# A window-attention and Fourier kernel: score buffers, first loads and score banks rearranged

## The chip, the cores and the metric

The kernel runs on one core of a Trainium2 chip. Everything is float32. The metric is the device time of one execution in microseconds (us), lower is better; before the change the runs shown have a median of 3386.23 us (3383.5 to 3388.03, three runs). The engines go by short names: PE is the matmul engine, DVE the vector engine, ACT the scalar engine, POOL is GpSimd, and SP issues DMAs. ACT and POOL can issue DMAs too. Matmul results land in PSUM, eight banks of 128 partitions by 512 floats, from where DVE and ACT evict them; POOL works on the main on-chip memory alone.

## What is computed

32 images of 56 x 56 tokens with 128 channels go through two residual layers, each behind a group normalization (32 groups of 4 channels).

```python
# layer 0: shifted-window attention, windows of 7 x 7, shift 3, 4 heads of 32 channels
x = x + L0(gn(x))
    xs   = roll(x, (-3, -3));  win = windows of 49 tokens, 8 x 8 of them an image
    q, k, v = win @ w_qkv.T                      # per head, q scaled by 32 ** -0.5
    attn = softmax(q @ k.T + bias[head] + mask[window])
    out  = roll((attn @ v) @ w_proj.T + b_proj, (3, 3))
# layer 1: Fourier mixing along both axes, then a feed-forward of 512
x = x + L1(gn(x))
    xy = idct(dct(x, W)[:32] mixed by w0);  xx = idct(dct(x, H)[:32] mixed by w1)
    out = relu((xx + xy) @ W1 + b1) @ W2 + b2
```

## The kernel before, in words

The program is one long loop over cycles. A cycle starts one row of eight windows, 392 tokens; eight rows make an image, so 256 rows in all. The order of the instructions on PE, ACT, DVE and POOL is written out by hand: what the loop calls first stands first on its engine, and each engine works strictly in that order. DMAs stand in their issuer's order.

**The attention of a row** is spread over several cycles. `attn_qk` (L393) makes the q and k products of row r in one PSUM bank each, and ACT evicts them, q once (L406) and k twice (L416, for even and odd heads). `attn_scores` (L438) makes 16 matmuls into two banks; DVE adds the bias and the mask while it evicts them into a score buffer `a` (L459). `attn_max` (L466) takes the row maximum on DVE (L469) and subtracts it on POOL (L470); `attn_exp` (L474) is one ACT instruction. `attn_recip` and `attn_divide` (L478, L486) sum and invert on DVE and divide on POOL, in six pieces (L495), into `blocks`; `attn_transpose` (L502) turns these on DVE into `eT` (L505). `attn_v` (L424) makes v of the row, evicted by ACT (L436). `attn_values` (L508) multiplies by v into two banks, evicted by ACT (L552) and DVE (L550). `attn_project` (L554) projects into one bank, and DVE adds the input rows while it evicts (L569) and SP stores the result to a scratch in memory. `attn_sums` (L579) forms group sums on DVE and squares on ACT (L593).

**PSUM.** There are two rings of banks, each handed out in turn: `pa` with four banks for the attention (L81) and `pc` with four for the Fourier layer and the feed-forward (L84). A tile from a ring may be written only when what was read from the same bank last has been read. In the steady part a cycle takes eight banks from `pa`, in this order: q, k, two for the values, two for the scores, v, projection.

**The opening.** Image 0 is loaded in eight DMAs, half by SP and half by ACT, each of 32 rows by 56 tokens by 32 channels (`load_columns_of`, L130); `turn_quarter` (L296) transposes it on DVE, a quarter at a time. Then come constants, the bias table (seven small DMAs into `rpb_cols`, seven more into `rpb`, one copy of it to the upper half of the partitions, L180 to L187), four mask DMAs (L195), and on DVE the sum of both, `bm` (`bias_and_mask`, L201, L205). `image_norm` (L336) is a chain of small DVE instructions with one POOL instruction, the inverse deviation (L377), from which ACT scales the weights (L385); every q product waits for that.

**The first rows.** For cycles 0 to 10 (`CONV_BEGIN` is 11) `first_rows` (L1031) sets the order. In cycle c it calls: q and k of row c, exponential of row c-1, values of row c-3, bias of the input rows, division of row c-1, transposition of row c-2, scores and maximum of row c, projection of row c-3, steps of the next image's normalization, sums of row c-4, loads, v of row c, the mask additions on POOL (cycles 4 and 5), and the next image's quarter.

**The steady part.** From cycle 11 on, `halves_first` (L894), `half_columns`, `eighths`, `quarters`, `behind_max` and `halves_last` (L1003) interleave the Fourier layer and the feed-forward of earlier images with the attention of row c. On PE a cycle runs q and k (in `halves_first`), the first feed-forward product, values, scores, pieces of the Fourier layer, v, more of these, the second feed-forward product, and last the projection (in `halves_last`); right behind it stand q and k of the next row. On DVE the eviction of the second feed-forward product (L811, whose input needs an addition by POOL, L783) stands ahead of the eviction of the projection (L569).

Of the kernel before, what the change touches and what calls it, by code (L numbers as in the profile page):

```python
# [14 lines left out]
P = 128  # L15
# [31 lines left out]
def swin_fourier_kernel(  # L47
# [30 lines left out]
    def bank(tag, bufs):  # L78
        return psum.tile([P, HB], F32, tag=tag, name=tag, bufs=bufs)

    def attn_bank():  # L81
        return bank("pa", 4)

    def conv_bank():  # L84
        return bank("pc", 4)
# [41 lines left out]

    HW = S // 2

    def load_columns_of(dst, b, k, w0, w1, both=False):  # L130
        rows = slice(k * (S - KB), k * (S - KB) + KB)
        for cb in range(C // KB):
            cs = slice(cb * KB, (cb + 1) * KB)
            (nc.scalar if both and cb % 2 else nc.sync).dma_start(dst[cs], x[b, rows, w0:w1, cs])

    def load_quarter(b, k, u):

        t = work.tile([P, HW, KB], F32, tag="xin", name="xin", bufs=1)
        load_columns_of(t, b, k, u * HW, (u + 1) * HW)
        return t  # L140

    xins = {}
    for k in range(2):
        first = big.tile([P, NM * S + JP - S], F32, tag="y", name="xin_first", bufs=2)
        first = first[:, : S * KB].rearrange("p (w c) -> p w c", w=S)
        load_columns_of(first, 0, k, 0, S, True)
        for u in range(2):
            xins[0, k, u] = first[:, u * HW : (u + 1) * HW]
    x1 = big.tile([TC, NCH, C], F32, tag="x1", name="x1")


# [19 lines left out]
    with nc.allow_non_contiguous_dma(reason="relative position bias, once"):  # L171


        cols = work.tile([P, 4, C], F32, tag="zT", name="rpb_cols").rearrange("p n c -> p (n c)")
        cols = cols[:WS, : NH * span * WS].rearrange("p (h y x) -> p h y x", h=NH, y=span)
        for ix in range(WS):
            src = bass.AP(
                rpb_rev.tensor, rpb_rev.offset + WS - 1 - ix, [[span, NH * span], [1, WS]]
            )
            (nc.scalar if ix % 2 else nc.sync).dma_start(  # L180
                cols[ix : ix + 1].rearrange("p h y x -> p (h y) x"), src.unsqueeze(0)
            )
        for iy in range(WS):
            nc.sync.dma_start(
                rpb[iy * WS : (iy + 1) * WS], cols[:, :, WS - 1 - iy : span - iy]
            )
    nc.sync.dma_start(rpb[JP : JP + WT], rpb[0:WT])  # L187
# [4 lines left out]
    for hh in range(2):  # L192
        rows = slice(hh * JP, hh * JP + WT)
        for k, src in enumerate((shift_mask[:, 0, 0:WT], shift_mask[:, 2, JP : JP + WT])):
            nc.sync.dma_start(mask_sb[rows, :, k], src.rearrange("r p j -> p r j"))  # L195
    NP = NWR // 2
    bm = const.tile([P, 2, 2, NP, 2, WT], F32, tag="bm", name="bm")
    nc.gpsimd.memset(bm, 0.0)
# [70 lines left out]
    nc.vector.memset(heads, 0.0)  # L269
    for h in range(NH):  # L270
        nc.vector.memset(heads[h * HD : (h + 1) * HD, h % 2 : h % 2 + 1], 1.0)
    q_sb = big.tile([P, RT + JP - WT], F32, tag="q", name="q")
    nc.gpsimd.memset(q_sb, 0.0)
    v_sb = [big.tile([P, NP, C], F32, tag=f"v{i}", name=f"v{i}") for i in range(3)]
    a_sb = [big.tile([P, NH, NP, WT], F32, tag=f"a{i}", name=f"a{i}") for i in range(2)]
    blocks = [
        big.tile([P, 2, NH * NP, KB], F32, tag=f"blocks{i}", name=f"blocks{i}") for i in range(2)
    ]
# [2 lines left out]

    class Image:
        pass
# [49 lines left out]
    def image_norm(im):  # L336
# [47 lines left out]
        )  # L384
        nc.scalar.mul(im.w, wqkv, rstd)  # L385
        yield
        pb = attn_bank()
        halved(pb[:, 0:1], wqkv[:, 2 * C :], nb)
        nc.vector.tensor_copy(im.bias[:, 2:3], pb[:, 0:1])
        yield  # L390
# [46 lines left out]

    def attn_scores(im, i, r):  # L438

        q, a = q_sb, a_sb[r % 2]  # L440

        ps = [attn_bank(), attn_bank()]
        for pr in range(NP):
            for hp in range(2):
                cs = HALVES[hp]
                for e in range(2):
                    w = 2 * pr + e  # L450
                    nc.tensor.matmul(  # L451
                        ps[hp][HALVES[e], pr * 2 * WT : (pr + 1) * 2 * WT],
                        lhsT=q[cs, w * WT : w * WT + JP],
                        rhs=k_sb[cs, :, w],
                        start=True,
                        stop=True,
                    )
        for hp in range(2):
            nc.vector.tensor_tensor(  # L459
                a[:, 2 * hp : 2 * hp + 2, :, 0:WT].rearrange("p u w j -> p w u j"),  # L460
                ps[hp][:, :RT].rearrange("p (w u j) -> p w u j", u=2, j=WT),
                bm[:, i // (NWR - 1), hp],
                ALU.add,
            )

    def attn_max(r):  # L466
        a3 = a_sb[r % 2].rearrange("p t w j -> p (t w) j")
        mx = small.tile([P, 2 * NWR], F32, tag="mx", name="mx")
        nc.vector.tensor_reduce(mx, a3, axis=AX.X, op=ALU.max)  # L469
        nc.gpsimd.tensor_tensor(  # L470
            a3, a3, mx.unsqueeze(2).to_broadcast([P, 2 * NWR, WT]), ALU.subtract
        )

    def attn_exp(r):  # L474
        a2 = a_sb[r % 2].rearrange("p t w j -> p (t w j)")
        nc.scalar.activation(a2, a2, AF.Exp)  # L476

    def attn_recip(r):  # L478
        a3 = a_sb[r % 2].rearrange("p t w j -> p (t w) j")
        sm = small.tile([P, 2 * NWR], F32, tag="sm", name="sm")  # L480
        nc.vector.tensor_reduce(sm, a3, axis=AX.X, op=ALU.add)  # L481
        rs = small.tile([P, 2 * NWR], F32, tag="rs", name="rs")
        nc.vector.reciprocal(rs, sm)  # L483
        return rs

    def attn_divide(r, rs):  # L486
        a3 = a_sb[r % 2].rearrange("p t w j -> p (t w) j")
        dst = blocks[r % 2]
        lo, hi = (slice(0, KB), slice(KB, JP)), (slice(JP, JP + KB), slice(JP + KB, P))
        halves = [(slice(0, P), slice(0, P), k, k) for k in range(2)]  # L490
# [115 lines left out]
            )  # L606

    def fourier_stats(im):
        pg = attn_bank()

        for k, t in enumerate((im.tot, im.part[:, NWR - 1])):
            t = t.rearrange("p k g -> p (k g)")
# [417 lines left out]

    def first_rows(cycle):  # L1031
        im, i = row(cycle)
        if im:
            attn_qk(im, i)
        if cycle:
            attn_exp(cycle - 1)
        im3, i3 = row(cycle - 3)
        if im3:
            attn_values(im3, i3, cycle - 3)
        tokens_bias(cycle)  # L1040
        divide(cycle)
        turn(cycle)
        if im:
            attn_scores(im, i, cycle)
            attn_max(cycle)
        if im3:
            attn_project(im3, i3)
        for _ in range(3 if cycle == NWR - 1 else cycle in (0, NWR)):
            norm_step(cycle)
        last, j = row(cycle - 4)  # L1050
        if last:
# [114 lines left out]
```

## Time and profile before

| what | value |
|---|---|
| median of the runs shown | 3386.23 us (3383.5 to 3388.03) |
| the profiled execution | 3378.94 us, of which the span 3377.1 us |
| granted PE clock, mean | 0.99 |
| chain that ended last | PE 78%, DVE 8%, POOL 5%, ACT 5%, issue 3%, DMA 1% |
| scores: L451, 32 matmul records a row | 8192, 251 ns each |
| eviction of scores: L459 | 512, 560 ns each |
| row maximum: L469 | 256, 967 ns each |
| subtraction on POOL: L470 | 256, 1508 ns each |
| exponential: L476 | 256, 855 ns each |
| division on POOL: L495 | 1536, 856 ns each |

The slices of the page show the opening as the only stretch in which PE isn't full:

```profile
PE   4689999999999999999999999999999999999999
PEld 2467777777878777777777777777777777777776
DVE  6778777777777777777778777777777778777641
ACT  2456665566655666666666665566665666665553
POOL 5777777677676777777777676677776777777641
PEclk8889999999999999999999999999999999999999
```

Each digit is a fortieth of the span (84 us) and gives the busy share in tenths; the last line is the clock that PE was granted. Matmuls are pipelined and their ends are modelled, so a busy PE says that there was always a matmul under way, not that each ran at its best.

### The profile page before, as it was taken

To read this page: it belongs to the slowest core of one execution; us is meant where nothing else is said; L and a number is where in the kernel's file an instruction comes from. 1 tells how busy PE (TensorE), PEld (TensorE's weight loads), DVE (VectorE), ACT (ScalarE), POOL (GpSimd) and SP (SyncE) were. 2 spreads that over 40 slices of the span, in tenths; PEclk is the share of its full clock that TensorE was granted. 3 is DMA by queue.
4 is the path that set the end of the run, shared out by engine and by line. 5 is a ranking of instruction groups with operands and counts; after the bars stand their busy time and mean duration, and the time that the engine had idled before them with its cause. 6 is when DMAs were issued, how large, how long until landed. Compare 5 with 4: busy or idle time off the path is not lost.

```text
span 3377.1 us, 158257 instructions
## 1 busy us (share of the span) xinstructions
PE 3252.4 (96%) x69504; PEld 2561.5 (76%) x69504; DVE 2468.8 (73%) x4793; ACT 1979.1 (59%) x3649; POOL 2334.6 (69%) x2724
## 2 busy tenths in 40 slices
PE   4689999999999999999999999999999999999999
PEld 2467777777878777777777777777777777777776
DVE  6778777777777777777778777777777778777641
ACT  2456665566655666666666665566665666665553
POOL 5777777677676777777777676677776777777641
PEclk8889999999999999999999999999999999999999
DMA  5546555556555555555556555555555655555443
GB/s 94 111 117 149 134 132 139 130 136 147 131 132 132 141 133 142 140 133 137 137 137 147 134 133 131 135 135 141 135 139 134 140 137 140 138 135 132 117 129 101
DMA packets 1158097, 448.85 MB, mean 133 GB/s; under 512 B 509951, under 2 KB 1127584, under 8 KB 1157408
## 3 DMA queue, kind: packets, MB, share of 16 engines
q1 hardware_dynamic: 1149565, 437.50, 54.2%
q8 instruction: 546, 8.95, 1.2%
q10 hardware_dynamic: 7843, 1.24, 0.3%
q14 instruction: 143, 1.17, 0.1%
HBM read 277.01 MB, written 161.48 MB: 130 GB/s over the span
## 4 chain that ended last, share of the span: by engine, by line
PE 78%; DVE 8%; POOL 5%; ACT 5%; issue 3%; DMA 1%; SPq 0%; DVEq 0%; POOLq 0%; ACTq 0%
PE pc L110 36%; PE pa L110 13%; PE pa L429 6%; PE pc L666 5%; PE pc L739 5%; PE pa L451 5%; PE pa L520 4%; PE pc L700 4%; POOL blocks L495 4%; ACT hid L776 2%; POOL a L470 1%; DVE eT L505 1%; DVE a L459 1%; DVE xw L308 1%; DVE st L329 1%
## 5 line engine op out<-in xcount | busy, mean ns | idle before, releaser
L495 POOL TENSOR_TENSOR blocks<-a,rs 32x512 f32<-32x512 f32 (+3 forms) x1536 | 1304.3, 856 | 646.9 <-DVE rs L483 542.4
L110 PE MATMUL pc<-wff,hid 128*64 128x128 f32 x12544 | 744.2, 273 | 2.5 <-issue 1.0
L110 PE MATMUL pc<-xf,wff 128*64 128x512 f32 (+2 forms) x3584 | 720.1, 539 | 1.1 <-DVE xf L750 0.9
L110 PEld LDWEIGHTS pc<-wff,hid 128*64 128x64 f32 x12544 | 705.0, 137 | 10.5 <-ACT hid L776 4.6
L110 PEld LDWEIGHTS pc<-xf,wff 128*64 128x64 f32 x3584 | 291.4, 136 | 344.1 <-issue 229.7
L470 POOL TENSOR_TENSOR a<-a,mx 128x784 f32<-128x784 f32 x256 | 386.0, 1508 | 235.4 <-DVE mx L469 202.5
L776 ACT ACTIVATE hid<-pc,b1sb 128x512 f32<-128x512 f32 (+2 forms) x896 | 512.9, 646 | 60.7 <-PE pc L110 52.6
L550 DVE TENSOR_SCALAR oT<-pa,bqkv 128x147 f32<-128x147 f32 (+2 forms) x768 | 171.1, 279 | 376.1 <-PE pa L520 376.1
L593 ACT ACTIVATE xr<-x 112x384 f32<-112x384 f32 (+1 forms) x256 | 147.1, 574 | 509.5 <-DVE x L569 509.5
L110 PE MATMUL pa<-xw,wn 128*64 128x392 f32 x2048 | 400.8, 500 | 41.3 <-ACT wn L385 36.2
L811 DVE TENSOR_TENSOR res<-pc,res 128x512 f32<-128x512 f32 (+3 forms) x257 | 143.0, 566 | 373.6 <-issue 168.3
L436 ACT COPY v<-pa 128x512 f32<-128x512 f32 x256 | 152.1, 594 | 356.4 <-PE pa L429 356.1
L783 POOL TENSOR_TENSOR res<-res,b2sb 128x512 f32<-128x512 f32 (+2 forms) x256 | 266.8, 1048 | 88.2 <-DMA res<-scr 88.2
L416 ACT ACTIVATE k<-pa,bqkv,heads 128x392 f32<-128x392 f32 x512 | 317.5, 673 | 2.3 <-PE pa L110 1.9
L476 ACT ACTIVATE a<-a 128x784 f32<-128x784 f32 x256 | 218.8, 855 | 170.4 <-POOL a L470 160.4
L505 DVE STREAM_TRANSPOSE eT<-blocks 128x1024 f32<-128x1024 f32 x256 | 315.7, 1233 | 0.0
L429 PE MATMUL pa<-wn,xw 128*64 128x128 f32 x4096 | 290.1, 283 | 15.9 <-issue 7.8
L124 POOL TENSOR_TENSOR xr<-xr,bproj 112x384 f32<-112x384 f32 (+1 forms) x256 | 292.5, 1142 | 7.4 <-DMA xr<-in_x_dram 7.3
L459 DVE TENSOR_TENSOR a<-pa,bm 128x392 f32<-128x392 f32 x512 | 265.2, 560 | 30.1 <-PE pa L451 6.5
L520 PEld LDWEIGHTS pa<-eT,v 49*32 49x32 f32 x16384 | 173.7, 106 | 146.5 <-issue 94.7
L110 PE MATMUL pa<-wproj,oT 128*48 128x128 f32 (+1 forms) x3584 | 253.3, 276 | 21.7 <-ACT oT L552 15.4
L481 DVE TENSOR_REDUCE sm<-a 128x16 f32<-128x784 f32 x256 | 245.2, 958 | 35.6 <-ACT a L476 35.5
(94 smaller groups left out, 5023.0 us busy)
## 6 DMA issues: line engine op xcount, KB each, us to landing
zscr<-z SPq DMA_DIRECT2D x512, 112.0 KB
xin<-in_x_dram SPq DMA_DIRECT2D x496, 112.0 KB
htok<-scr SPq DMA_DIRECT2D x256, 196.0 KB
zT<-zscr SPq DMA_DIRECT2D x192, 256.0 KB
res<-scr SPq DMA_DIRECT2D x160, 256.0 KB
out_dram<-res SPq DMA_DIRECT2D x160, 256.0 KB
scr<-x SPq DMA_DIRECT2D x128, 224.0 KB
xr<-in_x_dram SPq DMA_DIRECT2D x128, 168.0 KB
```

Source lines behind the costliest of these rows:

```text
L110: nc.tensor.matmul(dst[ps], lhsT=lhsT[:, ps], rhs=rhs, start=start, stop=stop)
L124: nc.gpsimd.tensor_tensor(piece, piece, bproj.unsqueeze(1).to_broadcast([TC, n, C]), ALU.add)
L416: nc.scalar.activation(k_sb[:, u], pk[:, :RT].rearrange("p (w j) -> p w j", j=WT), AF.Identity, bias=im.bias[:, 3 + u : 4 + u], scale=head ...
L429: nc.tensor.matmul(pv[HALVES[w % 2], w // 2 * C : (w // 2 + 1) * C], lhsT=im.half[i // NP][:, t0 : t0 + JP], rhs=im.w[:, 2 * C : 3 * C], s ...
L459: nc.vector.tensor_tensor(a[:, 2 * hp : 2 * hp + 2, :, 0:WT].rearrange("p u w j -> p w u j"), ps[hp][:, :RT].rearrange("p (w u j) -> p w u ...
L470: nc.gpsimd.tensor_tensor(a3, a3, mx.unsqueeze(2).to_broadcast([P, 2 * NWR, WT]), ALU.subtract)
L481: nc.vector.tensor_reduce(sm, a3, axis=AX.X, op=ALU.add)
L495: nc.gpsimd.tensor_tensor(dst[to, k, :, :n], a3[src, :, kb * KB : kb * KB + n], rs[src].unsqueeze(2).to_broadcast([src.stop - src.start, 2 ...
L505: nc.vector.transpose(eT.rearrange("p t (k j) -> p k t j", k=2), blocks[r % 2])
L520: nc.tensor.matmul(po4[u][h * HD : (h + 1) * HD, pr], lhsT=v[ks, pr, h * HD : (h + 1) * HD], rhs=eT[ks, h * NP + pr, :WT], start=True, sto ...
L776: nc.scalar.activation(hf[:, :n], ph[:, :n], AF.Relu, bias=b1sb[:, f : f + 1])
L783: nc.gpsimd.tensor_tensor(im.res[:m, c0:c1], im.res[:m, c0:c1], b2sb[:m].unsqueeze(1).to_broadcast([m, c1 - c0, C]), ALU.add,)
```

## The change

Five things are changed at once.

1. *Three score buffers in the first rows, and another order there.* A third buffer, `a_extra`, is laid into space that the loads of image 0 leave. Rows 0 to 8 go round three buffers, later ones round two. In `first_rows` the scores, the maximum with its subtraction, and now also the exponential of row c stand ahead of the division of row c-1. The mask additions move from POOL in cycles 4 and 5 to DVE in cycles 1 and 2, and two of image 1's normalization steps move from cycle 7 to the end of cycle 6.
2. *Image 0 in quarters.* Sixteen DMAs of half the size in place of eight.
3. *Small loads by GpSimd.* The bias table's and the mask's DMAs are issued by POOL in place of SP and ACT.
4. *Banks.* The scores get two banks of their own, `ps0` and `ps1`, cleared once; the ring `pa` goes from four banks to two. The two small products of the normalizations are taken from `pc`.
5. *49 weight columns.* The score matmuls load 49 columns of q in place of 64; the partitions between the windows stay zero from the one clearing, and q's tile loses its padding.

In the steady part the order of the calls is untouched. The built program places the first group of `bm` additions on DVE between the second and the third quarter of image 0, the second group between the third and the fourth, and POOL's DMAs between its clear of `bm` and its other clears.

```diff
     def attn_bank():
-        return bank("pa", 4)
+        return bank("pa", 2)
...
-    def load_columns_of(dst, b, k, w0, w1, both=False):
+    def load_quarter(b, k, u):
+        if b:
+            t = work.tile([P, HW, KB], F32, tag="xin", name="xin", bufs=1)
+        elif u:
+            t = others[k]
+        else:
+            t = big.tile([P, NM * S + JP - S], F32, tag="y", name="xin_first", bufs=2)
+            t = t[:, : S * KB].rearrange("p (w c) -> p w c", w=S)
+            others.append(t[:, HW:])
+            t = t[:, :HW]
         rows = slice(k * (S - KB), k * (S - KB) + KB)
         for cb in range(C // KB):
             cs = slice(cb * KB, (cb + 1) * KB)
-            (nc.scalar if both and cb % 2 else nc.sync).dma_start(dst[cs], x[b, rows, w0:w1, cs])
+            queue = nc.scalar if b == 0 and cb % 2 else nc.sync
+            queue.dma_start(t[cs], x[b, rows, u * HW : (u + 1) * HW, cs])
...
-            (nc.scalar if ix % 2 else nc.sync).dma_start(
+            nc.gpsimd.dma_start(
                 cols[ix : ix + 1].rearrange("p h y x -> p (h y) x"), src.unsqueeze(0)
...
-            nc.sync.dma_start(
+            nc.gpsimd.dma_start(
                 rpb[iy * WS : (iy + 1) * WS], cols[:, :, WS - 1 - iy : span - iy]
...
-    nc.sync.dma_start(rpb[JP : JP + WT], rpb[0:WT])
+    nc.gpsimd.dma_start(rpb[JP : JP + WT], rpb[0:WT])
...
-            nc.sync.dma_start(mask_sb[rows, :, k], src.rearrange("r p j -> p r j"))
+            nc.gpsimd.dma_start(mask_sb[rows, :, k], src.rearrange("r p j -> p r j"))
...
-    q_sb = big.tile([P, RT + JP - WT], F32, tag="q", name="q")
-    nc.gpsimd.memset(q_sb, 0.0)
+    q_sb = big.tile([P, RT], F32, tag="q", name="q")
...
+    def attn_buffer(r):
+        return a_sb[r % 3 if r < CONV_BEGIN - 2 else r % 2]
...
+    ps = [bank(f"ps{hp}", 1) for hp in range(2)]
+    for t in ps:
+        nc.vector.memset(t, 0.0)
...
-        pb = attn_bank()
+        pb = conv_bank()
...
-        ps = [attn_bank(), attn_bank()]
...
-                        ps[hp][HALVES[e], pr * 2 * WT : (pr + 1) * 2 * WT],
-                        lhsT=q[cs, w * WT : w * WT + JP],
+                        ps[hp][e * JP : e * JP + WT, pr * 2 * WT : (pr + 1) * 2 * WT],
+                        lhsT=q[cs, w * WT : (w + 1) * WT],
...
-        pg = attn_bank()
+        pg = conv_bank()
...
     def first_rows(cycle):
         im, i = row(cycle)
+        im3, i3 = row(cycle - 3)
         if im:
             attn_qk(im, i)
-        if cycle:
-            attn_exp(cycle - 1)
-        im3, i3 = row(cycle - 3)
         if im3:
             attn_values(im3, i3, cycle - 3)
         tokens_bias(cycle)
-        divide(cycle)
-        turn(cycle)
         if im:
             attn_scores(im, i, cycle)
             attn_max(cycle)
+            attn_exp(cycle)
+        divide(cycle)
+        turn(cycle)
...
-        for _ in range(3 if cycle == NWR - 1 else cycle in (0, NWR)):
+        for _ in range(cycle in (0, NWR - 1, NWR)):
             norm_step(cycle)
...
-        if cycle in (4, 5):
+        if cycle in (1, 2):
             for half in range(2):
-                bias_and_mask(nc.gpsimd, 1, cycle - 4, half)
+                bias_and_mask(nc.vector, 1, cycle - 1, half)
...
+        if cycle == NWR - 2:
+            for _ in range(2):
+                norm_step(NWR - 1)
...
         if cycle == CONV_BEGIN - 1:
             attn_sums(im3, i3)
-            attn_exp(cycle)
...
+        extra = big.tile([P, NM * S + JP - S], F32, tag="y", name="a_extra", bufs=2)
+        extra = extra[:, : NH * NP * WT].rearrange("p (t w j) -> p t w j", t=NH, w=NP)
+        a_sb.append(extra)
```

More of the change, by code (lines that the diff above doesn't have):

```diff
@@ L133, in load_columns_of @@
             cs = slice(cb * KB, (cb + 1) * KB)
-            (nc.scalar if both and cb % 2 else nc.sync).dma_start(dst[cs], x[b, rows, w0:w1, cs])
-    def load_quarter(b, k, u):
-        t = work.tile([P, HW, KB], F32, tag="xin", name="xin", bufs=1)
-        load_columns_of(t, b, k, u * HW, (u + 1) * HW)
+            queue = nc.scalar if b == 0 and cb % 2 else nc.sync
+            queue.dma_start(t[cs], x[b, rows, u * HW : (u + 1) * HW, cs])
         return t
-    xins = {}
+    xins, others = {}, []
     for k in range(2):
-        first = big.tile([P, NM * S + JP - S], F32, tag="y", name="xin_first", bufs=2)
-        first = first[:, : S * KB].rearrange("p (w c) -> p w c", w=S)
-        load_columns_of(first, 0, k, 0, S, True)
         for u in range(2):
-            xins[0, k, u] = first[:, u * HW : (u + 1) * HW]
+            xins[0, k, u] = load_quarter(0, k, u)
     x1 = big.tile([TC, NCH, C], F32, tag="x1", name="x1")
@@ L438, in attn_scores @@
     def attn_scores(im, i, r):
-        q, a = q_sb, a_sb[r % 2]
-        ps = [attn_bank(), attn_bank()]
+        q, a = q_sb, attn_buffer(r)
         for pr in range(NP):
@@ L466, in attn_max @@
     def attn_max(r):
-        a3 = a_sb[r % 2].rearrange("p t w j -> p (t w) j")
+        a3 = attn_buffer(r).rearrange("p t w j -> p (t w) j")
         mx = small.tile([P, 2 * NWR], F32, tag="mx", name="mx")
@@ L474, in attn_exp @@
     def attn_exp(r):
-        a2 = a_sb[r % 2].rearrange("p t w j -> p (t w j)")
+        a2 = attn_buffer(r).rearrange("p t w j -> p (t w j)")
         nc.scalar.activation(a2, a2, AF.Exp)
     def attn_recip(r):
-        a3 = a_sb[r % 2].rearrange("p t w j -> p (t w) j")
+        a3 = attn_buffer(r).rearrange("p t w j -> p (t w) j")
         sm = small.tile([P, 2 * NWR], F32, tag="sm", name="sm")
@@ L486, in attn_divide @@
     def attn_divide(r, rs):
-        a3 = a_sb[r % 2].rearrange("p t w j -> p (t w) j")
+        a3 = attn_buffer(r).rearrange("p t w j -> p (t w) j")
         dst = blocks[r % 2]
```

## The prediction

> **What bounds the kernel now.** I read the page's busy shares first, then the stretches, then the timeline of one image, then the opening 60 us.
>
> ```profile
> PE 3252.4 (96%) x69504; PEld 2561.5 (76%) x69504; DVE 2468.8 (73%) x4793; ACT 1979.1 (59%) x3649; POOL 2334.6 (69%) x2724
> ```
>
> ```profile
> 142.00:200.00 58.00, 44.11 (x966) 36.18 (x963) 46.42 (x93) 28.69 (x56) 41.80 (x50) 0.83 0.52 119
> 200.00:260.00 60.00, 54.98 (x1268) 42.93 (x1266) 45.64 (x86) 34.08 (x62) 41.99 (x51) 0.94 0.55 118
> 1600.00:1705.00 105.00, 104.74 (x2286) 80.99 (x2282) 81.42 (x161) 65.86 (x122) 76.00 (x88) 1.00 0.57 137
> ```
>
> The columns are stretch, length, then busy time of PE, weight loads, DVE, ACT and POOL, granted clock, DMA share, GB/s. In the middle of the run PE is busy 104.74 of 105 us at clock 1.00; only ahead of about 260 us does it idle. Two consequences. A wait put in front of PE in the steady part is paid in full; and work saved in the opening is worth its own length once.
>
> Now the seam between two window rows in the steady part: the projection of one row (PE, `pa<-wproj,oT`), its eviction (DVE L569), and the q and k products of the next row (PE, `pa<-xw,wn`, q first).
>
> ```profile
> 1625.55 1.04 PE L110 MATMUL pa<-wproj,oT 128*64 128x128 f32 x16
> 1626.42 1.49 PE L110 MATMUL pa<-xw,wn 128*64 128x392 f32 x8
> 1626.64 0.69 DVE L569 TENSOR_TENSOR x<-pa,xr 112x512 f32<-112x512 f32 x1
> ...
> 1645.83 1.04 PE L110 MATMUL pa<-wproj,oT 128*64 128x128 f32 x16
> 1646.70 1.49 PE L110 MATMUL pa<-xw,wn 128*64 128x392 f32 x8
> 1648.03 3.60 PE L110 MATMUL pc<-xf,wff 128*64 128x512 f32 x16
> ...
> 1648.14 0.42 DVE L811 TENSOR_TENSOR res<-pc,res 128x256 f32<-128x256 f32 x1 [1.22 <-POOL res L783]
> 1648.48 0.68 DVE L569 TENSOR_TENSOR x<-pa,xr 112x512 f32<-112x512 f32 x1
> ```
>
> Columns: start, duration, engine, line, operation. PE goes from one to the next without a gap, and the eviction runs beside the q and k products: it ends at 1627.33 and at 1649.16, while the k product starts 0.66 after the q product (an image's first row, where another matmul lies between the two, shows q at 1611.08 and that matmul at 1611.74), so at 1627.08 and 1647.36.
>
> **The change, part by part.**
>
> *Two shared banks in place of four.* A window row takes, in the steady order, banks for q, k, two value products, v and the projection: after the change six from a ring of two, as the score products have banks of their own. So q takes the bank that v left, k the one that the projection left. The k product must then wait for L569. Before, k took the bank of a score product, emptied long ago. The eight rows of the image above give, as end of L569 less start of k: 0.03, 0.25, 0.31, 1.80, 0.15, 0.25, 0.25, 0.60 us, 3.64 together. The 1.80 is DVE held for 1.22 by POOL's L783, ahead of L569. Over rows 24 to 255 (images 3 to 31), by the same subtraction, the mean is 3.36 per image. A release from DVE to PE adds its hop: a transpose that ends at 48.36 (47.17 + 1.19) lets PE start at 48.50, so 0.15 each, 1.2 per image. Behind k on PE stand the feed-forward, value and score products, and all wait too. What comes back: PE waits for ACT between scores and v in four of the eight rows, 0.11, 0.11, 0.11 and 0.23 us over the usual 0.73; ACT's backlog there shrinks when PE comes later, so I return 0.45 of these 0.56. Net 3.36 + 1.2 - 0.45 = 4.1 us per image, x 29 = **119 us**. Bounds: no hop and twice the return, 2.4 x 29 = 70; all of 3.64 + 1.2 and no return, 4.84 x 29 = 140. The other new waits are covered: q waits for v's copy on ACT, which ended 1.68 us or more ahead of q in every row from 24 on; the value products now wait for k's eviction, 0.1 to 1.9 us ahead of them, and k is late by no more than PE is. If that cover were gone, the tightest row would pay 0.1 us, 3 us in all.
>
> In rows 11 to 23 the subtraction gives 19.6 us, but PE was busy only 76% and 92% of the two stretches above. I count **6**; bounds 0 and 22 (with hops).
>
> The clock: the stretches grant 0.79 on average from 40 to 120 us, where PE idles for several us at a time, and 1.00 where it is dense; new waits of 0.2 to 1.9 us lie between, and I count no loss of clock. [...]
>
> *49 weight columns for the scores.* Per row 32 weight loads and 32 matmul records.
>
> ```profile
> L110 PE MATMUL pa<-wproj,oT 128*48 128x128 f32 x1792 | 243.1, 277 | 0.0
> L110 PE MATMUL pa<-wproj,oT 128*64 128x128 f32 x1792 | 242.1, 276 | 21.7 <-ACT oT L552 15.4 <-DVE oT L550 6.3
> ```
>
> The groups by shape show that 48 and 64 weight columns cost a matmul the same (277 and 276 ns, the number behind the busy time); only the load shortens, 124 against 139 ns, and PE hides loads. I take 0. If the score block of 0.73 us shrank by 15/64, it would give back 0.17 x 232 rows = 40 us; that is the other end.
>
> *Small loads by GpSimd.* Nineteen DMAs (7 bias columns, 4 masks, 7 rearrangements, 1 copy) go from SP and ACT to POOL, in its order behind `bm`'s clear (ends at 2.1) and ahead of its other clears and of L377, the inverse deviation that opens the matmuls. SP and ACT lose them, which nothing waits for. The two clears of the score banks on DVE fall before 9.97 us, where it waits for image 0 anyway (0.84 to 1.7 us is all it does there); without that cover they would cost about 1 us, by `blocks`' clears of 0.95 on POOL.
>
> ```profile
> 11.66 4.70 SPq L180 DMA_DIRECT2D rpb_cols<-in_rpb_rev_dram  x4
> 18.47 5.82 SPq L184 DMA_DIRECT2D rpb<-rpb_cols  x7
> ...
> 23.58 0.56 POOL L377 TENSOR_TENSOR rstd<-ve,mhalf 128x1 f32<-128x1 f32 x1 [19.01 <-DVE ve L373]
> ...
> 25.95 0.80 SPq L187 DMA_DIRECT2D rpb<-rpb  x1
> ```
>
> The additions into `bm` (L205, two groups of 1.45 us) now stand between image 0's quarters on DVE, so the transposes queue behind them and they behind POOL's DMAs. No row shows a DMA issued by POOL. With p for an issue: 18 issues end at 2.1 + 18p; 2.2 us of clears and landing, the copy p, its landing 2.6 (from 26.75 to the additions at 29.33); then 1.45 of additions, 1.8 and 2.0 of last quarter and statistics, 2.6 of normalization: L377 at 14.8 + 19p. Nearest row: SP issues the same transfers at 0.83 (5.82/7): 0.8 gives 30.0 against 23.58, a **loss of 6.4**. Bounds: at 0.25 (the shortest small load on SP) DVE's own work is the limit, near 25, a loss of 1.5; at 2.07 (the longest, image 0's loads, 8.27/4) it is 54, a loss of 30. Image 0 in quarters is inside this: transposes may begin up to 4 us ahead of 9.97, but they stand behind the additions.
>
> *First rows.* Before, score evictions follow each other at 9.24 and 9.31 us (57.51, 66.75, 76.06), with two long beats, 14.3 (76.06 to 90.33; a quarter's DMA awaited until 84.09, POOL adding masks for 2.9) and 15.9 (99.57 to 115.43; image 1's normalization). Afterwards POOL needs 8.4 per row (division 5.34, subtraction 1.50, 1.14 and 0.4 of small ones). But k of the next row now waits for v's copy, and ACT does that behind the exponential of the same row: k product 0.83, k on ACT 1.25, scores 0.91, eviction 1.00, maximum 0.97, subtraction 1.50, exponential 0.86, square 0.55, copy 0.58, and nine hops of 0.1 (0.05 behind ACT, 0.15 behind DVE in this trace) make 9.35. The third buffer and the earlier subtraction free POOL, which then isn't what the beat waits for. The ordinary beat stays. From the long beats I take **-5** (DMA and DVE still hold the first to about 12, the second to 11.5, less some 2 for DVE's added mask work). Bounds 0 and -14 (POOL's 8.4 on eight beats and 6.7 from the long ones).
>
> **Sum.** 119 + 6 + 6.4 - 5 = 126 us. The profiled execution took 3378.94 (span 3377.1); it becomes 3505. The median of the runs, 3386.23, lies 7.3 above it, so the forecast is 3386 + 126 = **3512 us**.
>
> **The rivals.** *Faster: the eviction is ahead of k.* Place: L569 against the k product. It decides if DVE ends L569 0.15 us ahead of k in all eight rows; the steady part then costs 0, and the opening counts: -14 + 1.5, 3374 us. For it: DVE is busy only 73%. Against: in five rows L569 starts within 0.1 us of its input's end and takes 0.55 to 0.69 itself, against 0.66 of q. 4%. *No change:* gain and loss would have to meet by chance; 2%. *Cover or columns:* PE catches up half of the wait (70 in place of 119) or the scores shrink (-40): 3460 to 3475. For it, the 0.56 of ACT waits and the shorter load; against, PE's missing gaps. 20%. *POOL's issues cost 2 us:* +24, 3536. For it, no row to say otherwise; against, SP's 0.83. 15%. *The forecast:* 59%, 3485 to 3545.
>
> **How the numbers follow.** Low end 3386 + 70 - 12 = 3444; high end 3386 + 140 + 22 + 30 = 3578, of which I keep 3445 to 3565. About 0.2% (7 us) is what a measurement of this kernel can tell from no change. Faster 0.04, same 0.02, slower 0.94.
>
> **What would show it.** Right: in the steady stretches PE has a gap of 0.2 to 2 us ahead of every second `pa<-xw,wn` product, released by DVE L569, and an image takes 104 to 106 us where it took 100 to 103; score matmuls keep their length; L377 comes near 30 us; score evictions still 9 to 10 us apart. Wrong: no such gap, or an image period unchanged; score blocks below 0.6 us; a first-row beat near 8.4.

## The result, and the profile after

| | before | changed |
|---|---|---|
| median | 3386.23 us | 3562.71 us (3559.57 to 3566.73) |
| ratio, with 95% interval | | 1.0522 [1.0507, 1.0538] |
| span of the profiled execution | 3377.1 us | 3557.8 us |
| granted PE clock, mean | 0.99 | 0.984 |

The changed kernel is slower by 176.5 us. First the busy shares on the page of the changed kernel:

```profile
PE 3328.0 (94%) x69504; PEld 2503.9 (70%) x69504; DVE 2487.2 (70%) x4811; ACT 2018.1 (57%) x3649; POOL 2337.7 (66%) x2726
```

PE has as many instructions as before, and still bounds the kernel, but its share fell from 96% to 94%. The same three stretches as before (columns as there):

```profile
142.00:200.00 58.00, 40.46 (x804) 29.93 (x806) 40.20 (x75) 26.11 (x46) 40.63 (x50) 0.77 0.48 104
200.00:260.00 60.00, 45.82 (x988) 33.85 (x984) 44.16 (x84) 30.47 (x57) 40.04 (x48) 0.85 0.46 114
1600.00:1705.00 105.00, 101.85 (x2160) 76.59 (x2158) 76.43 (x149) 62.57 (x114) 71.77 (x84) 1.00 0.55 131
```

In the steady stretch PE now idles 3.15 of 105 us where it idled 0.26, at an unchanged clock of 1.00; in the two early ones it is busy less (40.46 for 44.11, 45.82 for 54.98) and the clock fell as well, from 0.83 to 0.77 and from 0.94 to 0.85; earlier rows stand in them than before, as the kernel is late there. The seam between two rows, the place that the prediction names, for the rows that answer to those shown before:

```profile
1724.23 1.04 PE L110 MATMUL pa<-wproj,oT 128*64 128x128 f32 x16
...
1724.51 0.69 DVE L820 TENSOR_TENSOR res<-pc,res 128x512 f32<-128x512 f32 x1 [3.50 <-PE pc L110]
...
1725.11 1.84 PE L110 MATMUL pa<-xw,wn 128*64 128x392 f32 x8
...
1725.33 0.69 DVE L578 TENSOR_TENSOR x<-pa,xr 112x512 f32<-112x512 f32 x1
...
1726.07 0.20 PEld L110 LDWEIGHTS pa<-xw,wn 128*64 128x64 f32 x4 [0.82 <-DVE x L578]
...
1745.79 1.04 PE L110 MATMUL pa<-wproj,oT 128*64 128x128 f32 x16
...
1746.66 0.83 PE L110 MATMUL pa<-xw,wn 128*64 128x392 f32 x4
...
1747.77 0.42 DVE L820 TENSOR_TENSOR res<-pc,res 128x256 f32<-128x256 f32 x1 [1.21 <-POOL res L792]
...
1748.11 0.68 DVE L578 TENSOR_TENSOR x<-pa,xr 112x512 f32<-112x512 f32 x1
...
1748.84 0.88 PE L110 MATMUL pa<-xw,wn 128*64 128x392 f32 x4 [1.35 <-DVE x L578]
```

The eviction of the projection (L569 before, L578 now) ends at 1726.02 and the weights of k load at 1726.07; in the fourth row of the image it ends at 1748.79 and k starts at 1748.84, 2.18 us behind q in place of 0.66. The wait stands in every row; in the first of the two it is too short to split q and k into two records, and only the weight load shows it.

To see where the time went I compared the start of each row's first q product in two traces. That is worked out from the trace by row, not a line of the page:

| from the start to ... | row 0 | row 24 | row 248 | end |
|---|---|---|---|---|
| changed kernel later by (us) | 6.7 | 30.7 | 176.5 | 180.7 |
| the prediction's sum | 6.4 | 7.4 | 122 | 126 |

Rows 24 to 248 are 28 images and lost 145.8 us, 5.21 per image. There the time from the start of q to the start of k grew by 3.72 us per image (by row of the image 0.09, 0.32, 0.34, 1.48, 0.25, 0.30, 0.29, 0.65); the fourth row lost another 1.1 us elsewhere, and the remaining 0.4 is spread.

### The profile page after: what moved, and what is told of

Same layout as the page of the kernel before. It is cut to its first block, busy times and chain, and to the rows that moved or that the text cites. A ratio compares the mean times of both kernels' runs of the same rounds, so it can differ in the third digit from the quotient of the medians.

```text
span 3557.8 us, 158120 instructions
## 1 busy us (share of the span) xinstructions
PE 3328.0 (94%) x69504; PEld 2503.9 (70%) x69504; DVE 2487.2 (70%) x4811; ACT 2018.1 (57%) x3649; POOL 2337.7 (66%) x2726
## 4 chain that ended last, share of the span: by engine, by line
PE 77%; DVE 13%; issue 5%; POOL 2%; DMA 2%; ACT 1%; SPq 0%; DVEq 0%; ACTq 0%; POOLq 0%
PE pc L110 35%; PE pa L110 12%; PE ps L460 6%; PE pa L439 5%; PE pc L675 5%; PE pa L529 5%; PE pc L748 5%; PE pc L709 4%; DVE x L578 3%; DVE eT L514 2%; DVE a L468 2%; DVE mx L478 2%; DVE st L339 1%; POOL blocks L504 1%; DVE xw L318 1%
## 5 line engine op out<-in xcount | busy, mean ns | idle before, releaser
L504 POOL TENSOR_TENSOR blocks<-a,rs 128x512 f32<-128x512 f32 x1518 | 1289.4, 856 | 674.8 <-DVE rs L492 572.7
L110 PEld LDWEIGHTS pc<-wff,hid 128*64 128x64 f32 x12544 | 708.5, 137 | 10.3 <-ACT hid L785 4.6
L110 PE MATMUL pc<-xf,wff 128*64 128x512 f32 (+2 forms) x3584 | 712.6, 539 | 0.5 <-DVE xf L759 0.4
L110 PE MATMUL pa<-xw,wn 128*64 128x392 f32 x2048 | 462.5, 523 | 146.3 <-DVE x L578 70.4
L785 ACT ACTIVATE hid<-pc,b1sb 128x512 f32<-128x512 f32 (+2 forms) x896 | 529.6, 638 | 91.7 <-PE pc L110 87.5
L110 PEld LDWEIGHTS pc<-xf,wff 128*64 128x64 f32 x3584 | 253.3, 136 | 381.4 <-issue 304.1
L110 PEld LDWEIGHTS pa<-xw,wn 128*64 128x64 f32 x2048 | 126.0, 139 | 304.3 <-DVE x L578 227.9
L439 PE MATMUL pa<-wn,xw 128*64 128x128 f32 x4096 | 290.5, 282 | 10.4 <-issue 9.1
L468 DVE TENSOR_TENSOR a<-ps,bm 128x392 f32<-128x392 f32 x506 | 262.3, 560 | 45.7 <-PE ps L460 20.3
L439 PEld LDWEIGHTS pa<-wn,xw 128*64 128x64 f32 x4096 | 225.5, 138 | 49.1 <-issue 14.9
```

The lines of the kernel that those rows point to most:

```text
L110: nc.tensor.matmul(dst[ps], lhsT=lhsT[:, ps], rhs=rhs, start=start, stop=stop)
L439: nc.tensor.matmul(pv[HALVES[w % 2], w // 2 * C : (w // 2 + 1) * C], lhsT=im.half[i // NP][:, t0 : t0 + JP], rhs=im.w[:, 2 * C : 3 * C], s ...
L468: nc.vector.tensor_tensor(a[:, 2 * hp : 2 * hp + 2, :, 0:WT].rearrange("p u w j -> p w u j"), ps[hp][:, :RT].rearrange("p (w u j) -> p w u ...
L504: nc.gpsimd.tensor_tensor(dst[to, k, :, :n], a3[src, :, kb * KB : kb * KB + n], rs[src].unsqueeze(2).to_broadcast([src.stop - src.start, 2 ...
L785: nc.scalar.activation(hf[:, :n], ph[:, :n], AF.Relu, bias=b1sb[:, f : f + 1])
```

## The experiments

Differences in microseconds are against the median of the kernel before as it ran beside each: 3380.94 us for the first four, 3381.44 for loads, quarters, first rows and projection first, 3382.91 for the rest. "Row 24" and the like are shifts of the first q product in the profiled execution, "end" is the shift of its span.

**Banks alone.** The kernel before with

```
-        return bank("pa", 4)
+        return bank("pa", 2)
-        ps = [attn_bank(), attn_bank()]
+    ps = [bank(f"ps{hp}", 1) for hp in range(2)]   # once, ahead of the loop
-        pb = attn_bank()          # and pg
+        pb = conv_bank()
```

> The kernel before with the banks alone: two attention banks, two fixed score banks, pb and pg from the conv banks; still 64 weight columns, loads and first rows as before. Theory (the k product waits for the projection's eviction): the steady part loses what it lost in the changed kernel, 5.2 us per image x 28 = 146 us, and the opening some 5 to 15 of its 31 us, so 150 to 165 us over the kernel before (ratio 1.044 to 1.049). Rival (other parts of the change, GpSimd loads and the first rows' order among them, carry more than the opening, or the 49 columns cost time): less than 120 us (ratio below 1.036).

3547.06 us, ratio 1.0491 [1.0473, 1.0508], 166 us over the kernel before, just above the theory's 150 to 165. Steady growth 5.26 us per image, with the same pattern by row as in the changed kernel; row 24 is 20.2 us late. So the banks carry 166 of the 176 us, and more of the opening than I expected. (pb and pg are the small products of the first and the second normalization.) Row 13 shows the wait near its longest, first in the timeline (L570 is the eviction of the projection here), then in the stretches up to k, over k, and behind it:

```profile
166.61 0.87 PE L110 MATMUL pa<-xw,wn 128*64 128x392 f32 x4
...
170.99 0.67 DVE L570 TENSOR_TENSOR x<-pa,xr 112x512 f32<-112x512 f32 x1
...
171.71 1.57 PE L110 MATMUL pa<-xw,wn 128*64 128x392 f32 x4 [4.24 <-DVE x L570]
```

```profile
165.00:171.60 6.60, 2.48 (x36) 1.73 (x34) 6.57 (x12) 1.44 (x2) 4.97 (x7) 0.92 0.65 130
171.70:173.00 1.30, 1.29 (x4) 0.53 (x6) 1.26 (x3) 1.10 (x2) 0.03 (x1) 0.50 1.20 185
173.00:180.00 7.00, 6.97 (x184) 6.29 (x182) 3.39 (x8) 3.83 (x7) 5.05 (x6) 0.69 0.43 85
```

DVE is busy all the time (6.57 of 6.60), so the eviction starts 4.4 us behind q. PE idles 4.24 us, and behind that the granted clock is 0.50 and then 0.69: k takes 1.57 us where q took 0.87. If the lower clock comes of the wait, which no run here tests, this wait was paid twice.

**Banks and columns.** The same with `lhsT=q[cs, w * WT : (w + 1) * WT]`, 49 columns, and the cleared score banks.

> The kernel before with the banks and the 49 weight columns. Theory: the columns are worth 0.02 us per row as the score blocks of the two profiles show (0.71 against 0.73), 5 us in all, so within 0 to 8 us under the banks alone. Rival (the score block shrinks with its weight columns): 40 us under the banks alone. Rival (narrower weights keep rows of the bank from being written and cost nothing else): exactly the same as the banks alone.

3549.63 us, ratio 1.0495 [1.0479, 1.0510]: no difference from the banks alone. The rival of 40 us falls; 5 us and nothing can't be told apart.

**Banks and columns undone.** The changed kernel with four shared attention banks and 64 columns.

> The changed kernel with its banks and columns undone (four shared attention banks, 64 columns, padded q); the opening stays changed. Theory: no wait for the projection's eviction in the steady rows, and the opening keeps the 6.7 us of the GpSimd loads and what the first rows lose or gain without the ring of two: 0 to 15 us over the kernel before (ratio 1.000 to 1.005). Rival (the 31 us of the opening come from loads, order and VectorE beside GpSimd, not from the ring): 25 to 35 us over (ratio 1.008 to 1.010). Rival (something else than the ring holds the steady part): more than 60 us over.

3390.72 us, ratio 1.0027 [1.0017, 1.0038]. Steady growth falls from 5.21 to 0.27 us per image, row 24 from 30.7 to 5.2. So the banks carry 25.5 of the 30.7 us of the opening too (added alone, they gave 20.2), and the rest of the change costs about 10.

**Projection in a conv bank.** One line of the changed kernel: `pp = conv_bank()`.

> The changed kernel with one edit: the projection takes its bank from the four conv banks, so the k product takes the bank that v left and the q product one that the value products left; the ring stays at two. Theory (it is the projection's eviction that k waits for): the steady part goes back to 100 to 104 us per image, and 20 to 45 us over the kernel before remain (ratio 1.006 to 1.013). Rival (a ring of two is too short in itself, with the value products waiting for q and k and k for v's copy): at least 100 us over (ratio above 1.03).

3431.24 us, ratio 1.0151 [1.0135, 1.0167]. The projection now takes its bank from the other ring, `pc`. The fourth row of the image, the second of the two in the seam shown with the result:

```profile
1680.10 1.49 PE L110 MATMUL pa<-xw,wn 128*64 128x392 f32 x8
...
1681.42 3.60 PE L110 MATMUL pc<-xf,wff 128*64 128x512 f32 x16
...
1681.87 0.68 DVE L578 TENSOR_TENSOR x<-pc,xr 112x512 f32<-112x512 f32 x1
```

q and k run as one record again, and the eviction comes after both without holding anything. From q to k nothing grows any more (0.00 us in all eight rows), with the ring still at two: k waited for the projection's eviction, and a ring of two is not too short for q and k in the steady part. Steady growth is 1.06 us per image, though, 29.7 us in all, 0.93 of it in the fourth row, and the total is beyond what I expected. The theory lacked a term.

**Loads by GpSimd alone.** The kernel before with the 19 small loads issued by `nc.gpsimd`.

> The kernel before with one part of the change: the 19 small loads issued by GpSimd. Theory (the added shift of 6.7 us at the inverse deviation is GpSimd's issues, and it lasts): L377 near 30 us, first q product 5 to 7 us later than in the kernel before, 4 to 7 us over it at the end (ratio 1.001 to 1.002). Rival (the first rows absorb it): less than 2 us at the end. Rival (image 0 in quarters made the additions into bm stand in the way, not the issues): first q product less than 2 us later.

3389.80 us, ratio 1.0028 [1.0018, 1.0039]. First q product 9.4 us later, row 24 10.1, end 10.3: it lasts to the end, and costs more than the theory had.

**Quarters alone.** The kernel before with image 0 loaded in quarters.

> The kernel before with one part of the change: image 0 loaded in quarters, so that the first transposes begin near 6.5 us in place of 10. Theory: VectorE's own work behind the last quarter sets the inverse deviation, so that the first q product comes 1 to 3.5 us earlier and the run ends 0 to 4 us earlier. Rival (the last quarter's landing sets it, which does not move): first q product within 0.5 us of the kernel before.

3377.27 us, ratio 0.9994 [0.9985, 1.0003]. First q product 2.1 us earlier, end of the span 2.4: as expected, though the times can't tell it from no change. In between, row 3 is 2.2 us later.

**First rows alone.** The kernel before with three score buffers and the new order.

> The kernel before with one part of the change: three score buffers in the first rows and their new order, with four shared banks. Theory, from the changed kernel with four banks, where the shift of 6.7 us at row 0 was 5.2 at row 24 after a top of 13.1 at row 3: a loss of some 6 us in the first three rows (VectorE adds the second masks beside GpSimd's division), a gain of some 8 later, 1 to 3 us earlier at row 24 and at the end. Rival (the prediction's own number): 5 us earlier or more, up to 14. Rival (the order costs the first rows time and gives none back): later by 3 us or more.

3381.38 us, ratio 1.0003 [0.9994, 1.0013]; row 3 is 6.7 us later, row 24 0.8 earlier. Nothing, and not the 5 us of the prediction. By the ratios, the three parts make 0.25%, 8.5 us, and undoing the banks left 0.27%, 9.1 us; by the ends of the spans, of one execution each, it is 10.3 - 2.4 - 0.6 = 7.3 and 12.2. So the parts add up as far as this can tell.

**Projection first.** The changed kernel with

```
-            last_out(cycle)
             attn_project(im, j)
+            last_out(cycle)
```

> The changed kernel with two calls exchanged at the end of a cycle: the projection and its eviction stand ahead of the feed-forward's second product and L820, on TensorE and on VectorE. The ring stays at two and k still takes the projection's bank. Theory (k comes before L578 only because the projection is the last thing on TensorE): in the seven rows of an image that have a second product it lies between projection and q, the gap between q and k vanishes there and stays in one (0.65 us, the rows ahead of phase 7); 85 to 120 us under the changed kernel (ratio to the kernel before 1.017 to 1.027). Rival (a wait for L578 moves to the second product's bank, or the projection waits for oT instead): less than 40 us under the changed kernel (ratio over 1.040).

3456.55 us, ratio 1.0224 [1.0210, 1.0238], about 100 us under the changed kernel. The seam ahead of the fourth row now has the second product (`pc<-wff,hid`) between projection and q:

```profile
1692.11 1.04 PE L110 MATMUL pa<-wproj,oT 128*64 128x128 f32 x16
...
1692.99 1.92 PE L110 MATMUL pc<-wff,hid 128*64 128x128 f32 x32
...
1694.73 1.73 PE L110 MATMUL pa<-xw,wn 128*64 128x392 f32 x8
1694.88 0.65 DVE L578 TENSOR_TENSOR x<-pa,xr 112x512 f32<-112x512 f32 x1
```

The growth from q to k is gone in five rows, 0.04 and 0.09 in the third and fourth, and unchanged (0.65) in the eighth, ahead of which there is no second product. Bank and ring are as in the changed kernel; what differs is the place of the projection on PE and of its eviction on DVE. The fourth row still grows by 1.13 us.

**pg in a conv bank alone.** The kernel before with `pg = conv_bank()`.

> The kernel before with one edit: pg, the bank of an image's second statistics, comes from the conv banks, where it is the fifth bank behind the four of the feed-forward's first product. Theory (this, and not the ring of two, makes the growth of 0.9 to 1.1 us in the fourth row of an image that remains with the projection's bank or place changed): that row grows by 0.8 to 1.1 us, 25 to 30 us in all, ratio 1.007 to 1.009. Rival (the growth belongs to the ring of two, or to code that PE waits for): under 0.2 us in that row, ratio 0.998 to 1.002.

3406.52 us, ratio 1.0066 [1.0051, 1.0081]. The fourth row grows by 1.09 us, all others by nothing: 1.06 per image and 27.7 us at the end. This has the size and the place of the missing term. The kernel before in that row:

```profile
1648.03 3.60 PE L110 MATMUL pc<-xf,wff 128*64 128x512 f32 x16
...
1651.33 2.43 ACT L776 ACTIVATE hid<-pc,b1sb 128x512 f32<-128x512 f32 x4
...
1651.46 0.29 PE L110 MATMUL pa<-tot,gmean 112*64 112x64 f32 x4
```

And this run:

```profile
1660.89 3.60 PE L110 MATMUL pc<-xf,wff 128*64 128x512 f32 x16
...
1664.19 2.43 ACT L776 ACTIVATE hid<-pc,b1sb 128x512 f32<-128x512 f32 x4
...
1664.99 0.23 PEld L110 LDWEIGHTS pc<-tot,gmean 112*64 112x64 f32 x4 [1.38 <-issue]
1665.02 0.34 PE L110 MATMUL pc<-tot,gmean 112*64 112x64 f32 x4 [0.53 <-POOL blocks L495]
```

The feed-forward's first product fills all four conv banks, and pg is the fifth. Row by row in the trace, ACT's first of the four evictions ends at 1664.88, and pg's weights load 0.11 us later. The timeline names POOL's division as the releaser, but pg doesn't read what it writes, and in all 28 images the load comes 0.113 to 0.114 us behind the end of that eviction; so it is ACT that pg waits for. The wait is 0.53 us here and 0.36 in the mean. Most of the rest of the growth are gaps of PE in the Fourier blocks of the same row, 0.30 and 0.26 us more than before in the mean, at one product in one image and at another in the next, to which the profile gives no releaser. Why these grow stays open.

**pg back in the ring of two.** The run with the projection in a conv bank, and `pg` and `pb` from `attn_bank()`.

> The changed kernel with the projection's bank from the conv banks (as in the run that brought it to 50 us over the kernel before), and pg and pb back in the ring of two. Theory (pg behind the feed-forward's four banks costs the fourth row its 0.93 us): that row grows by no more than 0.4 us, steady growth 0.1 to 0.5 us per image in place of 1.06, 15 to 25 us under the run with the projection alone (ratio 1.007 to 1.010). Rival (the ring of two costs that row the same wherever pg lies, or pg in the ring makes the value products wait for VectorE): 1.0 us per image or more, ratio 1.014 or more.

3442.58 us, ratio 1.0172 [1.0159, 1.0186]: the theory's number missed. The fourth row grows by 0.64 in place of 0.93, but the first by 0.56, where pb now stands in the ring, and the steady growth is 1.51 us per image. pb itself now waits 0.40 us, where among the conv banks its row grew by 0.01; pg's own wait (0.31) is gone, but the gaps in the Fourier blocks of its row stay. So pg's bank explains the fourth row only in part once the ring has two banks, and pb is better off among the conv banks.

**Second masks early.** The kernel before with quarters and the new first rows, the second masks' additions put behind row 0's maximum:

```
+        if cycle == 0:
+            for t in range(2):
+                for half in range(2):
+                    bias_and_mask(nc.vector, 1, t, half)
-        if cycle in (1, 2):
...
```

> The kernel before with the image in quarters and the first rows in their new order, and with the second masks' 16 additions on VectorE behind row 0's maximum, where GpSimd only subtracts, in place of rows 1 and 2, where it divides. Theory (the loss of 6.7 us up to row 3 is these additions beside GpSimd's division): the top at row 3 is below 2 us, and the run ends 5 to 10 us under the kernel before (ratio 0.997 to 0.9985). Rival (the new order itself delays rows 1 to 3): the top stays near 6 us and the run ends 0 to 4 us under it.

3377.07 us, ratio 0.9982 [0.9973, 0.9990]: 5.8 us under the kernel before, the lowest ratio here. The time is the theory's, its sign is not: the q product of row 3 is still 6.0 us late, as the rival said. I think that the sign was badly chosen, for the score evictions of row 3 start at 54.46, against 59.63 in the run of the first rows alone and 57.51 before. Of these 5.2 us the quarters may have given 1.4 (row 0: 30.21 against 31.58), which would leave 3.8 for the place of the additions; since the interval reaches to 0.9990, a gain below 4 us isn't excluded.

**No copy.** The same, with the bias written to both halves by SP and ACT, and the masks issued by GpSimd.

> The one above, and the position bias written to both halves of its tile by seven DMAs each from SP and ACT, so that the copy from one half to the other and its landing fall away; the four masks are issued by GpSimd, idle there from 4.6 us on. Theory (row 0's additions wait for that copy until 29.3 us in the kernel before): additions 2 to 5 us earlier, scores of row 0 as much, and 2 to 4 us more at the end than the one above gives. Rival (row 0 waits for its k, or the rows absorb it): within 1 us of the one above.

3380.35 us, ratio 0.9989 [0.9980, 0.9998], nothing gained: first q product 1.7 us later than before, where the run above was 2.1 earlier, and row 0's additions end at 29.2 where they ended at 30.2. It is 3.3 us over the run above, more than the rival's 1 us, but the intervals overlap; so all that is shown is that the theory's gain didn't come.

## Why the prediction was right, and where its sizes were off

*The time: near the top of the range, and there by luck.* 3562.71 us are 51 over the forecast of 3512, outside the 3485 to 3545 that had a chance of 59%, and 2.3 under the kept top of 3565. The range reached so far for a longer steady wait, for rows 11 to 23 and above all for slow issues of GpSimd (30 us), and the issues weren't slow. The missing time came mostly from two losses that have no term in the sum, a second one in the fourth row of an image and the ring's in the rows ahead of row 11. By the profiled spans, of one execution each, the sum is 54.7 us short (180.7 less 126): 23.3 up to row 24, 31 in the 28 images behind it.

*Direction, place and chain of causes: right.* The k product waits for the eviction of the projection. Taking the bank away from that pair (projection in a conv bank) or moving the two apart (projection first) removed the wait in eight rows of eight and in five of eight (two more nearly), with the ring still at two.

*The steady wait, 4.1 us per image: right, partly by luck, as its errors compensate.* Measured directly, q to k grew by 3.72. Its first term, the subtraction over the old trace (3.36), held. The hop from DVE to PE was 0.055 us, not 0.15: L578's end to k's start, the median of 224 steady rows. The 0.15 was read behind a transpose; in the same trace of the kernel before PE starts 0.056 us behind L569 itself, in the three early rows where it waits for it. So the hops are 0.44 rather than 1.2, and 3.36 + 0.44 = 3.80; of the 0.45 that I returned for ACT's backlog at most 0.08 shows. Setting the changed kernel against the run with the projection in a conv bank gives 145.8 - 29.7 = 116.1 us over 28 images, 4.15 each, which holds some 0.4 that is not in the gap itself.

*What is missing from the sum: pg.* The diff moves pg and pb to the conv ring, and the prediction followed only the shrunken ring; it never asked what stands ahead of them in the ring that they join. By the run of that edit alone this is 1.06 us per image, 29.6 over the 28 images and nearly all of the 31 by which the sum fell short there. In the changed kernel pg itself doesn't wait, as PE is late already; the row's other 1.1 us lie mostly in a gap of the transforms. That it is the same loss is inferred from its size and place in three runs, not shown: with the projection in a conv bank, pg and pb back in the ring of two took the fourth row's growth only from 0.93 to 0.64.

*Rows 11 to 23, "I count 6": a little too small, and the rows ahead of them left out.* The banks cost 25.5 us up to row 24 (30.7 less 5.2). Row 11 starts 20.0 us late, and 3.4 with the banks undone; so 16.6 of the 25.5 fall ahead of row 11, where the prediction gave the ring no price, and 8.9 in rows 11 to 23 (with the banks alone 8.3 and 12.0). In rows 11 to 23 the time from q to k grew by 19.8 us in all, as its subtraction said (19.6), and about half of that fitted into idle time. Ahead of row 11 PE idles too, but there the chain that ended last runs through q, k, scores and the softmax of each row, and the waits are in it. Half of the 25.5 (12.6 us, 30.7 less the 18.1 of the projection in a conv bank) is L578. Of the rest v's copy is the largest wait: between 40 and 260 us PE idles 25.8 us for it ahead of q and k products, 4.5 before and none with the banks undone. In rows 1 and 2 it looks like this:

```profile
50.50 4.47 DVE L208 TENSOR_TENSOR bm<-rpb,mask 49x98 f32<-49x98 f32 x8
...
50.96 5.65 POOL L504 TENSOR_TENSOR blocks<-a,rs 128x512 f32<-128x512 f32 x6
...
51.03 0.86 ACT L485 ACTIVATE a<-a 128x784 f32<-128x784 f32 x1 [5.30 <-POOL a L479]
51.80 0.57 ACT L446 COPY v<-pa 128x512 f32<-128x512 f32 x1
...
52.42 0.88 PE L110 MATMUL pa<-xw,wn 128*64 128x392 f32 x4 [1.99 <-ACT v L446]
```

These are lines of the changed kernel's timeline: exponential, copy and product in a chain. The prediction named this chain and its beat, 9.35 us; the score evictions of rows 0 to 2 are 9.36 and 9.32 apart, later ones 9.4 to 16.9. With four banks the first beat is 7.6, but the second is 9.3 there too, so only the first shows the chain. The new order can run faster, and the ring of two takes that back; the prediction saw the second and not that it costs.

*First rows, -5: wrong in size.* -0.6 with four banks. In the run of the first rows alone the second long beat fell from 15.9 to 10.4 as assumed, but the first stayed (14.1 for 14.3), a third one ahead of row 11 grew from 15.0 to 17.5, and the term "some 2 for DVE's added mask work" was too small: eight additions take 4.47 us next to the division, where they take 1.45 in the opening.

*Loads by GpSimd, 6.4 with the quarters: right in sum, by luck.* L387 ran at 30.29, forecast 30.0. Most issues cost 0.55 and not 0.8 (the masks 0.71 to 0.77), by the rows of the changed kernel:

```profile
2.08 3.84 POOL L183 DMA_DIRECT2D rpb_cols<-in_rpb_rev_dram  x7
5.90 0.77 POOL L198 DMA_DIRECT2D mask<-in_shift_mask_dram  x1
8.21 2.13 POOL L198 DMA_DIRECT2D mask<-in_shift_mask_dram  x3 [1.54 <-DMA rpb_cols<-in_rpb_rev_dram]
12.19 3.78 POOL L187 DMA_DIRECT2D rpb<-rpb_cols  x7 [1.85 <-DMA rpb_cols<-in_rpb_rev_dram]
```

But POOL stops twice for a DMA, 3.4 us that the formula had not; and the loads cost 9.4 alone, of which the quarters give back some 2.7.

*The columns, 0, and the clock, no loss:* right in the steady part. The score products took 252 ns each (251 before) with 49 columns, though their weight loads fell from 133 to 121 ns, and the run with the columns shows no gain. The clock is 1.00 in the steady stretch, with added waits of 0.1 to 1.5 us in each row. In the opening the clock did fall, by 0.06 to 0.09 in the two stretches shown, and to 0.50 behind the wait of 4.24 us in the run with the banks alone; how much of the 25.5 us that is was not measured, and the prediction, which named low clocks there, gave them no price.

## What to carry to other kernels

When a ring of buffers is shortened, write down for each taker which tile it now follows, and when that tile is last read; the dangerous pair is the last product of one round and an early one of the next, and putting other work between them (or giving one of them another ring) takes the wait away. Do the same for the ring that a tile is moved into: the price can lie there. Idle time of the bounding engine is a poor cover for a new wait that lies in the chain that makes it idle: here about half of the waits of rows 11 to 23 was paid all the same, and the rows ahead of them lost more.

## What the runs showed of the hardware

VectorE's additions into `bm` took longer beside GpSimd's work than in the opening of the changed kernel, where eight of them take 1.45 us while GpSimd computes nothing. The timeline of the run with the second masks early:

```profile
32.17 4.43 DVE L208 TENSOR_TENSOR bm<-rpb,mask 49x98 f32<-49x98 f32 x16
...
32.33 1.61 POOL L476 TENSOR_TENSOR a<-a,mx 128x784 f32<-128x784 f32 x1 [10.30 <-DVE mx L475]
```

Twice 1.45 would be 2.90 for the 16; they took 1.53 longer, nearly the one subtraction (1.61) that fell into them. In the changed kernel, next to the six pieces of a division (5.65), eight of them took 4.47 in place of 1.45. Why they take longer there no run here shows. The prediction had used the price without a neighbour.

A second one: a rearrangement took 0.54 us to issue on GpSimd (7 in 3.78) and 0.83 on SP (7 in 5.82), a bias column 0.55 (7 in 3.84) and 1.18 (4 in 4.70); but a mask took 0.71 to 0.77 on GpSimd and 0.45 on SP, by this row of the kernel before:

```profile
16.48 1.81 SPq L195 DMA_DIRECT2D mask<-in_shift_mask_dram  x4
```

The shorter issues still delayed the first q product by 9.4 us in the run of the loads alone. VectorE's additions into `bm` waited there for the DMAs, and the last transposes of image 0 stood behind them:

```profile
19.71 1.45 DVE L205 TENSOR_TENSOR bm<-rpb,mask 49x98 f32<-49x98 f32 x8 [3.69 <-DMA rpb<-rpb_cols]
...
23.40 1.48 DVE L205 TENSOR_TENSOR bm<-rpb,mask 49x98 f32<-49x98 f32 x8 [2.24 <-DMA rpb<-rpb]
24.89 1.09 DVE L308 STREAM_TRANSPOSE xw<-xin_first 128x512 f32<-128x512 f32 x1
```

A third: in the kernel before PE did not start equally soon behind all of VectorE's instructions. It started 0.147 to 0.148 us behind the end of a transpose (L505, three waits) or of L550 (two), and 0.055 to 0.056 behind L459, L569 and L750 (eight).
